# A two-layer graph network on one core: attention masks made by two DMAs, one bias added by an accumulating DMA, weights fetched through a ring

## The chip, the cores and the metric

The kernel runs on one core of one Trainium2 chip. Its time is the device time of one execution in microseconds. The core has five engines that each work through their own queue in order: TensorE (PE in the profile, its weight loads are PEld), VectorE (DVE), ScalarE (ACT), GpSimd (POOL) and SyncE (SP, which here only issues DMAs). DMAs are issued from SP's queue and from POOL's queue.

## The reference

There are 32 graphs of 512 nodes with 256 features, and one 0/1 adjacency matrix of 512x512 per graph, given as int32, in which one entry in 32 is set. Two layers follow each other, each of a graph part and a feed-forward part, all with layer norm in front and a residual sum behind:

```python
# layer 0
x = x + relu(xn @ W_upd + (adj^T @ (xn @ W_msg)) / degree + bias)
t = max over d of (xn[d] + Wt[:, d]) + bt                  # tropical product, 1024 units
fused = g * pieces(t) + (1 - g) * gelu(xn @ Wc + bc)       # g = sigmoid(xn @ Wg + bg)
x = x + fused @ Wd + bd
# layer 1
score[i, j] = leaky_relu(src[i] + dst[j]) where adj[i, j] is 1, else excluded   # 4 heads of 64
x = x + layer_norm(relu(softmax_j(score) @ h + bias) + h) * gamma + beta
x = x + slice_mixer(xn)                                    # softmax to 64 slices x 8 heads, a scan, back
```

What matters below: layer 1's attention needs the mask of each graph with the node j of the sum on the partitions, that is `adj` transposed; and `bd`, the last bias of layer 0, is one row of 256 that is added to every node.

## The kernel before

**Layer 0** (`layer0_sorted`, lines 98 to 702). The graph convolution of each graph loads `adj` by a casting DMA from POOL's queue (line 392). The tropical product is not computed in full: rows are sorted by how many features can still win, and for each such feature a row of a table in DRAM is fetched by an indirect DMA on POOL's queue (lines 564 and 595, 128 rows of 4 KB each) and taken into a running maximum on DVE (line 598). `sums(s, g)` does this for a group of four tiles of 128 rows; there are 32 groups. Its last step adds `bd`, held in SBUF on all partitions, to the group's rows `xg`: four POOL instructions of 128x256 (line 610). `mixed` is the matmuls of the feed-forward part (line 623) and its pieces (lines 628 to 641), and `down` is the last product, added to `xg` (line 654) and stored to `x2s` (line 655, SP's queue).

**Layer 1** (`layer1_plain`, lines 865 to 1611) is a generator. Its setup is woven into the last groups of layer 0 by `woven`, a step at a time. The setup loads and transposes the weights: `load_T` (line 999) loads 128 rows of a weight by SP's queue into one of two buffers, transposes them on PE (line 1009) and copies them out on ACT (line 1010); there are 21 such steps. The last setup steps are `masks(0)`.

`masks(b)` (line 1080) makes the mask of graph b in four tiles of 128 rows. For each tile SP loads 256 KB of int32 (line 1086), ACT casts it to bf16 with a sum (line 1100) and squares it in place with a sum (line 1101), PE transposes four blocks of 128x128 (line 1091), and DVE copies them out of PSUM as uint8 (line 1092). The two sums serve the check at the end of `layer1_plain` (lines 1607 to 1611): every entry must be 0 or 1, and every row must have an edge. A flag that is raised there makes `tile_kernel` run both layers again in a plain form (line 2212).

`prepare(b)` (line 1155) gathers the rows of graph b (line 1161), runs `masks(b)` in between, norms (line 1173), adds a row by an accumulating DMA (`add_rows`, line 949, POOL's queue), makes the projections `hp` (line 1187), and brings the factors of the nodes i onto all partitions by way of DRAM: `ownd` (line 1204) and four loads `own` (line 1207), all on SP's queue. It has 15 steps (`STEPS`). `weigh` (line 1215) makes the attention weights on DVE: `max(own, other) * mask`, 16 instructions of 128x512 for each graph (line 1220). `attention(b)` (line 1223) multiplies them on PE: for each j, 8 products `avp` (line 1256), then 4 row sums `adp` (line 1261), in the order of the heads. While graph b is attended, `prepare(b + 1)` is woven in, and the slice mixer of the two graphs before runs beside both, at a pace (`PACE`, line 896) that is worked out from `TURNS`, `STEPS` and `WANTED`.

The order within each engine's queue is not the order of the source alone: the framework moves instructions of the same queue past one another where no data forbids it, and gives each DMA one of eight completion counters per kind of queue, which it waits for when it is used again.

Of the kernel before, what the change touches and what calls it, by code (L numbers as in the profile page):

```python
# [8 lines left out]
F32 = mybir.dt.float32  # L9
F32R = mybir.dt.float32r  # L10
I32 = mybir.dt.int32
BF16 = mybir.dt.bfloat16
# [7 lines left out]
P = 128  # L20
# [77 lines left out]
def layer0_sorted(tc, ident, eps, x, adj, w, x2s, ranks, over, following):  # L98
# [29 lines left out]
    with ExitStack() as ctx:  # L128
# [12 lines left out]
        bd = const("bd", [P, D], w["bd"].partition_broadcast(P))  # L141
# [35 lines left out]

        table = dr.tile([D, FFN], F32, tag="table", name="table", bufs=1)
# [364 lines left out]
        def feed_forwards():  # L543


            def sums(s, g):
# [62 lines left out]
                for t in range(NT):  # L609
                    nc.gpsimd.tensor_add(xg[:, t, :D], xg[:, t, :D], bd)  # L610
# [254 lines left out]
def layer1_plain(tc, ident, eps, x2s, ranks, adj, w, out, over, ps):  # L865
# [24 lines left out]
    STEPS = 15  # L890
# [10 lines left out]
    with ExitStack() as ctx:  # L901
# [16 lines left out]
        identb = cst.tile([P, P], BF16, tag="identb", name="identb")  # L918
        nc.vector.tensor_copy(identb, ident)
# [32 lines left out]
        edges = ctile("edges", [P, 2, B * NT])  # L952
# [44 lines left out]
        with tc.tile_pool(name="raw", bufs=2, side="right") as raw:  # L997

            def load_T(dst, src, name):

                R, Ccols = src.shape
                for r0 in range(0, R, P):
                    n = min(P, R - r0)
                    t = raw.tile([P, Ccols], F32, tag=f"raw{Ccols}", name=f"{name}_{r0}")
                    nc.sync.dma_start(t[:n], src[r0 : r0 + n, :])
                    pt = psum("tp", f"{name}p{r0}").rearrange("p (c r) -> p c r", r=P)
                    cs = Ccols // P
                    for c in range(cs):
                        nc.tensor.transpose(pt[:, c, :n], t[:n, c * P : (c + 1) * P], ident[:n, :n])
                    nc.scalar.copy(dst[:, :, r0 : r0 + n], pt[:, :cs, :n])  # L1010
                    yield

            yield from load_T(wfxT, w["W_fx"], "wfx")
            yield from load_T(inT, w["hy_in_w"], "in")
            yield from load_T(hoT, w["hy_out_w"], "ho")
            yield from load_T(owT, w["out_w"], "ow")
            yield from load_T(fcT, w["hy_fcD_w"], "fc")
# [5 lines left out]
            def twice_T(src, name):  # L1023

                R, Ccols = src.shape
                t = raw.tile([P, 2, Ccols], F32, tag="twice", name=name)
                for i in range(2):
                    nc.sync.dma_start(t[:R, i, :], src)
                pt = psum("tp", f"{name}p")
                nc.tensor.transpose(pt[:, :R], t[:R].rearrange("p i c -> p (i c)"), ident[:R, :R])  # L1030
                return pt


            wsT = raw.tile([P, G], F32, tag="wsT", name="wsT")
            nc.vector.tensor_copy(wsT, twice_T(w["W_slice"], "ws")[:, :G])
            wx = raw.tile([P, KC, D], F32, tag="wx", name="wx", bufs=1)
            nc.sync.dma_start(wx, w["W_x"].rearrange("(k p) d -> p k d", p=P))
            bx = raw.tile([P, KC], F32, tag="bx", name="bx")
            nc.sync.dma_start(bx, w["b_x"].rearrange("(k p) -> p k", p=P))
            bsl = raw.tile([1, H, G], F32, tag="bsl", name="bsl", bufs=1)  # L1040
            bs = raw.tile([1, G], F32, tag="bs", name="bs")
            nc.sync.dma_start(bs, w["b_slice"].rearrange("(o n) -> o n", o=1))
# [22 lines left out]
            for c in range(DC):  # L1065
                sq = raw.tile([P, H * G], F32, tag="wsl2", name=f"wsl2_{c}")
                nc.vector.tensor_mul(sq, wsl[:, c, :], wsl[:, c, :])
                nc.tensor.matmul(pn, ones, sq, start=c == 0, stop=c == DC - 1)
# [9 lines left out]
        masked = {}  # L1078

        def masks(b, bank="any"):  # L1080

            a, raw = [], []

            def load(t):
                raw.append(se.tile([P, N], I32, tag="ai", name=f"ai{b}_{t}", bufs=2))
                nc.sync.dma_start(raw[t], adj[b, t * P : (t + 1) * P, :])

            def turn(t):
                pt = ps.tile([P, NT, P], BF16, tag=bank, name=f"maskp{b}_{t}")
                for j in range(NT):  # L1090
                    nc.tensor.transpose(pt[:, j, :], a[t][:, j * P : (j + 1) * P], identb)
                nc.vector.tensor_copy(mask[:, :, t * P : (t + 1) * P], pt)

            load(0)
            load(1)
            yield
            for t in range(NT):
                n = b * NT + t
                a.append(se.tile([P, N], BF16, tag="a", name=f"a{b}_{t}", bufs=3))
                nc.scalar.activation(a[t], raw[t], AF.Identity, accum_out=edges[:, 0, n : n + 1])  # L1100
                nc.scalar.activation(raw[t], raw[t], AF.Square, accum_out=edges[:, 1, n : n + 1])
                if t + 2 < NT:
                    load(t + 2)
                if t == 1:
                    mask = se.tile([P, NT, N], mybir.dt.uint8, tag="mask", name=f"mask{b}")
                    yield
                if t > 1:
                    turn(t - 2)
                    yield
            for t in range(NT - 2, NT):  # L1110
                turn(t)
                yield
            masked[b] = mask

        yield from masks(0, "mm")
# [39 lines left out]
        def prepare(b):  # L1155
# [12 lines left out]
            edged = masks(b) if b not in masked else range(3)  # L1168
            for i, _ in enumerate(edged):
                if i < 3 or b not in masked:  # L1170
                    yield
                if i == 2:
                    normed(xt, xn, f"c{b}")
                    add_rows(xt, 0)
                    yield
# [5 lines left out]
            ht = sb.tile([P, NT, AH * HO], F32, tag="ht", name=f"ht{b}")  # L1181
            other = sb.tile([P, NT, AH], F32, tag="other", name=f"other{b}")
# [40 lines left out]
        def attention(b):  # L1223
# [21 lines left out]
            for i, (q, j) in enumerate(turns):  # L1245
# [5 lines left out]
                if q + 1 == AP:  # L1251
                    ends = dict(start=j == 0, stop=j == NT - 1)
                    for p in range(AP):
                        for k in range(2 * HO // HW):
                            h, e = 2 * p + k * HW // HO, k * HW % HO
                            nc.tensor.matmul(pv[p][k * HW : (k + 1) * HW, :], hv[:, j, h, e : e + HW],  # L1256
                                             weighed[b, h, j], **ends)
                    if j == 0:
                        pd = psum("pv", f"adp{b}")
                    for h in range(AH):  # L1260
                        nc.tensor.matmul(pd[h * HW : (h + 1) * HW, :], hv[:, j, h, HO:].to_broadcast([P, HW]),
                                         weighed.pop((b, h, j)), **ends)
# [14 lines left out]
            nc.vector.tensor_scalar_max(rs, dt.rearrange("p (t h e) -> p t h e", t=NT, h=AH)[:, :, :, 0], 1e-30)  # L1277
            nc.vector.reciprocal(rs, rs)
# [329 lines left out]
        nc.vector.tensor_sub(flags, edges[:, 1, :], edges[:, 0, :])  # L1608
        nc.vector.tensor_scalar(flags, flags, 0.0, None, ALU.not_equal)
        nc.vector.tensor_scalar(edges[:, 0, :], edges[:, 0, :], 0.5, None, ALU.is_lt)  # L1610
        nc.vector.tensor_add(flags, flags, edges[:, 0, :])
# [635 lines left out]
```

## Time and profile before

| what | us |
|---|---|
| median of three runs | 4365.9 (4364.42 to 4366.94) |
| the profiled execution, its own time | 4372.35 |
| its span, first to last instruction | 4370.6 |
| PE busy | 3882.4 (89% of the span) |
| DVE busy | 3279.3 (75%) |
| ACT busy | 2295.0 (53%) |
| POOL busy | 1617.9 (37%) |

The span is read as four stretches: layer 0 until about 1860 us after its start; the last groups of layer 0 with the setup of layer 1 woven in, until about 2340; the passage, until about 2520; and layer 1 proper, in which two graphs take some 120 us and which ends at 4370.6. A group's "idle before" is time in which its engine stood still ahead of it, with what ended the wait. Busy times of different engines overlap and do not add up to the span.

### The profile page before, as it was taken

How to read it: one execution, taken by the hardware profiler on the slowest of the kernel's cores; microseconds unless marked ns; L12 is line 12 of the kernel's file. 1: busy time of each engine (PE TensorE's matmuls, PEld its weight loads, DVE VectorE, ACT ScalarE, POOL GpSimd, SP SyncE). 2: the span in 40 equal slices, each digit the busy share in tenths (PEclk: the TensorE clock that was granted, in tenths of full speed). 3: DMA queues.
4: the chain of work that ended last, by engine and by line, in shares of the span. 5: the costliest groups of instructions: out<-in, count | busy, mean ns of one | idle time of the engine just before them, and what ended most of it. 6: DMA issues, size and time to landing. Idle time of an engine off the chain costs nothing.

```text
span 4370.6 us, 57973 instructions
## 1 busy us (share of the span) xinstructions
PE 3882.4 (89%) x20311; PEld 2456.1 (56%) x20311; DVE 3279.3 (75%) x7008; ACT 2295.0 (53%) x4756; POOL 1617.9 (37%) x2036
## 2 busy tenths in 40 slices
PE   5567898988989999888998899999999999999997
PEld 4454565565655666554555455655555555555555
DVE  6668887898878978877775777777777777777763
ACT  3345655566655656546564555555554455554533
POOL 2346644665536644354431322222222222222210
PEclk8778999999999999998999999999999999999998
DMA  5546543564436644375441322222222322222200
GB/s 128 160 154 216 179 156 126 165 218 143 153 117 199 199 156 135 93 250 167 147 133 40 95 73 73 69 65 72 68 68 76 78 75 78 64 74 77 61 25 21
DMA packets 244051, 507.52 MB, mean 116 GB/s; under 512 B 39299, under 2 KB 114827, under 8 KB 243748
## 3 DMA queue, kind: packets, MB, share of 16 engines
q0 software_dynamic: 107904, 349.50, 26.7%
q1 hardware_dynamic: 135844, 154.21, 11.3%
q8 instruction: 162, 2.65, 0.2%
q14 instruction: 141, 1.16, 0.1%
HBM read 446.46 MB, written 57.17 MB: 115 GB/s over the span
## 4 chain that ended last, share of the span: by engine, by line
DVE 33%; PE 32%; DMA 11%; issue 9%; POOL 8%; ACT 5%; SPq 0%; another core or an unknown queue 0%; DVEq 0%; POOLq 0%; ACTq 0%
DVE att L1220 4%; DVE acc L637 4%; PE clsp L623 4%; PE gatep L623 3%; PE po L652 3%; PE avp L1256 3%; DMA rows<-table,xs 2%; DVE best L598 2%; DMA rows<-table,tops 2%; DVE sw L1349 2%; DVE sst L1347 2%; PE yTp L1354 2%; DVE sw L1344 2%; PE oTp L1542 1%; DMA best<-table,xs 1%
## 5 line engine op out<-in xcount | busy, mean ns | idle before, releaser
L623 PE MATMUL clsp<-xnT,wc 128*128 128x512 f32 x1024 | 521.8, 628 | 55.5 <-ACT cls L625 39.7
L623 PE MATMUL gatep<-xnT,wg 128*128 128x512 f32 x1024 | 502.1, 609 | 10.5 <-ACT gate L625 9.7
L652 PE MATMUL po<-wd,acc 128*128 128x256 f32 x2048 | 456.9, 382 | 6.5 <-DVE acc L641 3.5
L652 PEld LDWEIGHTS po<-wd,acc 128*128 128x128 f32 x2048 | 388.8, 191 | 73.1 <-issue 9.2
L1220 DVE SCALAR_TENSOR_TENSOR att<-own,other,mask 128x512 f32<-128x512 f32 x512 | 366.1, 744 | 76.4 <-DMA own<-ownd 76.4
L637 DVE SCALAR_TENSOR_TENSOR acc<-past,fld,acc 128x512 f32<-128x512 f32 x448 | 346.3, 776 | 28.3 <-ACT past L636 20.3
L598 DVE SCALAR_TENSOR_TENSOR best<-rows,xs,best 128x1024 f32<-128x1024 f32 x212 | 273.1, 1290 | 121.4 <-ACT best L592 75.8
L632 ACT ACTIVATE acc<-tz,fld 128x512 f32<-128x512 f32 x256 | 199.0, 778 | 269.1 <-PE tz L630 237.5
L623 PEld LDWEIGHTS gatep<-xnT,wg 128*128 128x128 f32 x1024 | 197.3, 197 | 254.0 <-issue 200.8
L636 ACT ACTIVATE past<-tz,fld 128x512 f32<-128x512 f32 x448 | 291.6, 694 | 73.6 <-DVE acc L637 72.1
L595 POOL DMA_INDIRECT rows<-table,xs x212 | 247.3, 1166 | 176.7 <-DVE best L598 121.8
L1256 PE MATMUL avp<-att,hv 128*32 128x512 f32 x2048 | 297.4, 599 | 6.1 <-DVE att L1220 6.1
L623 PEld LDWEIGHTS clsp<-xnT,wc 128*128 128x128 f32 x1024 | 182.6, 199 | 195.2 <-issue 114.3
L434 PE MATMUL pm<-h,adj 128*128 128x258 f32 (+1 forms) x1024 | 178.9, 321 | 100.3 <-DVE keep L427 34.4
L625 ACT ACTIVATE gate<-gatep,fld 128x512 f32<-128x512 f32 x256 | 175.6, 686 | 153.4 <-PE gatep L623 130.4
L1342 PE MATMUL lgp<-wsl,x4T 128*128 128x512 f32 x512 | 241.4, 610 | 14.3 <-ACT sw L1343 6.7
L1354 PE MATMUL yTp<-sw,x 128*128 128x512 f32 x512 | 237.0, 602 | 17.4 <-DVE sw L1349 16.9
L1161 POOL DMA_INDIRECT x<-x2s,ranks x128 | 135.2, 1056 | 295.5 <-DVE att L1220 147.5
L553 POOL DMA_INDIRECT xs<-rows_of,order x128 | 158.8, 1241 | 229.7 <-DVE acc L637 111.8
L1307 POOL TENSOR_TENSOR mu<-mu,eps 128x16 f32<-128x16 f32 x32 | 111.3, 3478 | 350.4 <-DVE mu L1306 350.4
L1574 PE MATMUL outp<-v,swT 128*128 128x256 f32 x1024 | 227.6, 381 | 0.0
L625 ACT ACTIVATE cls<-clsp,fld 128x512 f32<-128x512 f32 x256 | 176.3, 689 | 94.4 <-PE clsp L623 59.1
(598 smaller groups left out, 8809.0 us busy)
## 6 DMA issues: line engine op xcount, KB each, us to landing
adj<-in_adj POOLq DMA_DIRECT2D x128, 256.0 KB
ai<-in_adj SPq DMA_DIRECT2D x128, 256.0 KB
x<-added POOLq DMA_DIRECT2D x64, 512.0 KB
own<-ownd SPq DMA_DIRECT2D x128, 256.0 KB
rows_of<-keep SPq DMA_DIRECT2D x32, 550.0 KB
x<-in_x SPq DMA_DIRECT2D x32, 512.0 KB
x2s<-xs SPq DMA_DIRECT2D x32, 512.0 KB
out<-x SPq DMA_DIRECT2D x32, 512.0 KB
```

The source lines that it names most:

```text
L595: nc.gpsimd.indirect_dma_start(out=row, out_offset=None, in_=table, in_offset=bass.IndirectOffsetOnAxis(ap=idxs[:, k : k + 1].bitcast(U32) ...
L598: nc.vector.scalar_tensor_tensor(m, row, vals[:, k : k + 1], m, ALU.add, ALU.max)
L623: nc.tensor.matmul(pf, wf[:, c, f * P : (f + 1) * P], xnT[:, c, :], start=c == 0, stop=c == DC - 1)
L625: nc.scalar.activation(o, pf, fn, bias=fld[:, f, bf : bf + 1], scale=1.0 if fn == AF.Gelu else 0.5)
L636: nc.scalar.activation(r, z, AF.Relu, bias=fld[:, f, AT + b : AT + b + 1])
L637: nc.vector.scalar_tensor_tensor(y, r, fld[:, f, CH + b : CH + b + 1], y, ALU.mult, ALU.add)
L652: nc.tensor.matmul(po[:, i, :], acc[f][:, t * P : (t + 1) * P], wd[:, f, :], start=f == 0, stop=f == FC - 1)
L1220: nc.vector.scalar_tensor_tensor(e, own[h], other[:, j, h : h + 1], mask[:, j, :], ALU.max, ALU.mult)
L1256: nc.tensor.matmul(pv[p][k * HW : (k + 1) * HW, :], hv[:, j, h, e : e + HW], weighed[b, h, j], **ends)
L1342: nc.tensor.matmul(pf, xnT[:, c, t * P : (t + 1) * P], wsl[:, c, :], start=c == 0, stop=c == DC - 1)
L1354: nc.tensor.matmul(py, xn[:, t, c * P : (c + 1) * P], sw[:, t, :], start=t == 0, stop=t == NT - 1)
L1574: nc.tensor.matmul(po[:, :D], swT[:, k, t * P : (t + 1) * P], v[:, k, :], start=k == 0, stop=k == KC - 1)
```

## The change

Four edits, made together.

1. **Masks.** `masks` is gone, with its loads, casts, squares, transposes and copies. In its place `shorten(b)` copies the adjacency matrix of a graph from DRAM to DRAM by one DMA on POOL's queue that casts int32 to bf16 (1 MB read, 0.5 MB written), two graphs ahead and kept in the program's order; and `turn(b)` fetches it by one transposing DMA on SP's queue into a bf16 mask of 128x4x512. The check becomes one ACT instruction for each graph, the square of (mask - 0.5) over 128x2048 with a sum, which must be 512 on every partition, and one DVE instruction of 128x4 that looks for a row sum of the attention that is zero. `STEPS` is 12.
2. **Order in attention.** The 8 products and the 4 row sums of a step are issued from the last head to the first.
3. **bd.** It is copied four times into a row of DRAM, and each group adds it by one accumulating DMA of 128x4x256 on POOL's queue.
4. **Weights.** The weight rows of layer 1 go through a ring of five buffers that is filled three pieces ahead, and four small tensors are loaded before them.

```diff
-        bd = const("bd", [P, D], w["bd"].partition_broadcast(P))
+        bd = dr.tile([NT, D], F32, tag="bd", name="bd", bufs=1)
+        nc.sync.dma_start(bd, w["bd"].partition_broadcast(NT))
...
-                for t in range(NT):
-                    nc.gpsimd.tensor_add(xg[:, t, :D], xg[:, t, :D], bd)
+                nc.gpsimd.dma_start(xg[:, :, :D], bd.partition_broadcast(P), accum_op=ALU.add)
...
-    STEPS = 15
+    STEPS = 12
...
-            yield from load_T(wfxT, w["W_fx"], "wfx")
-            yield from load_T(inT, w["hy_in_w"], "in")
-            yield from load_T(hoT, w["hy_out_w"], "ho")
-            yield from load_T(owT, w["out_w"], "ow")
-            yield from load_T(fcT, w["hy_fcD_w"], "fc")
+            def fetch(i):
+
+                _, src, r0 = pieces[i]
+                n = min(P, src.shape[0] - r0)
+                t = raw.tile([P, DI], F32, tag="piece", name=f"piece{i}", bufs=5)
+                nc.sync.dma_start(t[:n, : src.shape[1]], src[r0 : r0 + n, :])
+                return t
+
+            coming = [fetch(i) for i in range(3)]
+            yield
+            for i, (dst, src, r0) in enumerate(pieces):
+                if i + 3 < len(pieces):
+                    coming.append(fetch(i + 3))
+                n, cs = min(P, src.shape[0] - r0), src.shape[1] // P
+                pt = psum("tp", f"piecep{i}").rearrange("p (c r) -> p c r", r=P)
+                for c in range(cs):
+                    nc.tensor.transpose(pt[:, c, :n], coming[i][:n, c * P : (c + 1) * P], ident[:n, :n])
+                nc.scalar.copy(dst[:, :, r0 : r0 + n], pt[:, :cs, :n])
+                yield
...
-        yield from masks(0, "mm")
+        short, masked = {}, {}
+
+        def shorten(b):
+
+            if b < B:
+                short[b] = dr.tile([N, N], BF16, tag="short", name=f"short{b}", bufs=3)
+                tc.keep_in_program_order(nc.gpsimd.dma_start(short[b], adj[b], max_dma_last_dim=8192))
+
+        def turn(b):
+
+            if b < B:
+                masked[b] = se.tile([P, NT, N], BF16, tag="mask", name=f"mask{b}")
+                nc.sync.dma_start_transpose(masked[b], short.pop(b))
+
+        for b in range(2):
+            shorten(b)
+            yield
+        turn(0)
...
-            edged = masks(b) if b not in masked else range(3)
-            for i, _ in enumerate(edged):
-                if i < 3 or b not in masked:
-                    yield
-                if i == 2:
-                    normed(xt, xn, f"c{b}")
-                    add_rows(xt, 0)
-                    yield
+            if b:
+                turn(b)
+            shorten(b + 2)
+            yield
+            yield
+            yield
+            normed(xt, xn, f"c{b}")
+            add_rows(xt, 0)
+            yield
...
             ht = sb.tile([P, NT, AH * HO], F32, tag="ht", name=f"ht{b}")
+            nc.scalar.activation(ht.rearrange("p t e -> p (t e)").bitcast(BF16), mask.rearrange("p t n -> p (t n)"),
+                                 AF.Square, bias=centre, accum_out=edges[:, b : b + 1])
...
-                    for p in range(AP):
-                        for k in range(2 * HO // HW):
+                    for p in reversed(range(AP)):
+                        for k in reversed(range(2 * HO // HW)):
...
-                    for h in range(AH):
+                    for h in reversed(range(AH)):
...
+            nc.vector.tensor_scalar(edges[:, B + b * NT : B + (b + 1) * NT],
+                                    dt.rearrange("p (t e) -> p t e", t=NT)[:, :, 0], 0.0, None, ALU.is_le)
```

## The prediction

> **What bounds the kernel now.** I read the busy time by stretch first, then the groups by line and form, the waits, the chain of waits, and last the SP and DVE timelines around one graph. The stretches (columns: length, PE, PEld, DVE, ACT, POOL busy with instructions, PE clock, DMA share, GB/s):
>
> ```profile
> 300.00:1860.00 1560.00, 1389.03 (x5548) 908.04 (x5547) 1294.39 (x2618) 915.76 (x1572) 839.21 (x1123) 0.96 0.51 162
> 1860.00:2000.00 140.00, 116.16 (x438) 72.63 (x437) 101.36 (x137) 70.65 (x115) 76.05 (x65) 0.87 0.68 230
> ...
> 2520.00:4200.00 1680.00, 1609.38 (x10865) 974.95 (x10865) 1246.80 (x2805) 862.53 (x2212) 420.62 (x385) 1.00 0.26 70
> ```
>
> Layer 1 proper is PE's: 1609 of 1680 us, 96%, against 74% for DVE, 51% for ACT, 25% for POOL and a DMA share of 0.26. Layer 0 is nobody's alone: PE 89%, DVE 83%, POOL 54%, DMA 51%. Between 1860 and 2000 us PE falls to 83%. The groups that the change removes, and the accumulating DMA that stands as a model for the new one:
>
> ```profile
> L1091 PE MATMUL maskp<-identb,a 128*128 128x128 bf16 x512 | 45.4, 220 | 13.9 <-ACT sw L1343 8.5 <-DVE mask L1092 4.5 <-ACT a L1100 0.9
> L1092 DVE CAST mask<-maskp 128x512 uint8<-128x512 bf16 x128 | 85.8, 676 | 0.4
> L1100 ACT ACTIVATE a<-ai 128x512 bf16<-128x512 int32 x128 | 80.6, 630 | 94.5 <-PE maskp L1091 70.0 <-PE outp L1574 13.6 <-DMA ai<-in_adj 10.7
> L1101 ACT ACTIVATE ai<-ai 128x512 int32<-128x512 int32 x128 | 81.6, 638 | 1.2
> L610 POOL TENSOR_TENSOR xs<-xs,bd 128x256 f32<-128x256 f32 x128 | 109.3, 859 | 165.9 <-ACT xn L574 164.8
> L949 POOL DMA_DIRECT2D x<-added x64 | 59.5, 930 | 260.4 <-ACT x L1140 129.8 <-ACT hv L1140 117.8 <-ACT avT L1273 10.1
> ```
>
> On PE the masks cost little beside the matmuls, on DVE and ACT more. How much of this sets the end is read from the chain between 3000 and 3130 us (start, us, what):
>
> ```profile
> 3010.86 0.33 PE maskp L1091 x4
> ...
> 3026.12 0.67 PE maskp L1091 x12
> ...
> 3075.53 0.60 DVE mask L1092
> ...
> 3081.95 0.60 DVE mask L1092
> ...
> 3089.96 0.60 DVE mask L1092
> ...
> 3093.18 0.56 DVE mask L1092
> ```
>
> Six mask pieces, 3.36 us in 130, lie on it. Over the whole span the chain gives DMA 11% and POOL 8%:
>
> ```profile
> DVE 33%; PE 32%; DMA 11%; issue 9%; POOL 8%; ACT 5%; SPq 0%; another core or an unknown queue 0%; DVEq 0%; POOLq 0%; ACTq 0%
> ```
>
> **What the Trainium skill says.** (1) "DMA: Bandwidth & Descriptors", section SWDGE vs HWDGE vs iDMA: a cast or an accumulate needs GpSimd's queue, a transpose SP's or ACT's. The trace agrees as far as it goes: line 392's casts and line 949's accumulates are POOL's. No transposing DMA is in it. (2) The same page, Queues, rings and completion order: SP owns one ring on each DMA engine, and on an engine descriptors are consumed in order. So an `own` load issued behind a transposing DMA comes after it. (3) "VectorE: DVE Perf Modes", The three transpose paths: 390 ns for a block of 128x128 on TensorE, 1309 ns by DMA. The trace has 220 ns for PE's, 56 ns apart within a run (12 in 0.67 us).
>
> **The masks, removed.** For one graph 16 transposes, 4 copies, 8 ACT instructions with their sums, 4 loads. On the chain 3.36 us in 130 us are 3.1 us for two graphs (some 120 us), and with 30 of the 31 graphs made in this stretch that is 15 x 3.1 = 47 us. PE alone gives the same size: 512 x 0.056 = 29 us if only the pitch counts, 45.4 + 13.9 = 59 us with its own busy time and the idle before it. I take 47. Late next are PE's own matmuls and DVE's `att`. ACT loses 128 x (0.630 + 0.638) and two sums of about 0.2 each, some 213 us. It is not the bound, and PE's weight loads waited only 7.5 (`yTp`) and 10.9 us (`gp`) for its casts: I take -5 (0 to -18).
>
> **The masks, new work.** ACT: a row of 512 takes 0.63 us and one of 1024 takes 1.05 (line 1303), so 2048 come to about 1.9 + 0.2: 32 x 2.1 = 67 us of ACT, covered by its 49% idle; without the cover it is 67. DVE: 32 comparisons of 0.15 us, 5 us, set against 86 that leave. `att` reads bf16 in place of uint8; I leave its 0.74 us. POOL: 32 casting DMAs at 0.57 to 0.93 us of issue are 18 to 30 us. POOL's part of the chain is 8% of 4370 = 350 us of 1618 busy, 22%, so +6; it stands ahead of the next gather, the norms and `hv`. The casting DMA moves what the four `ai` loads moved, so its DMA time replaces theirs.
>
> **The transposing DMA** is the open price. From below: 0.5 MB at the 261 GB/s which the DMA page (Latency and other measured facts) gives, 2 us. From above: 16 blocks x 1.309 = 21 us if they follow each other; with 3.4 us to land, as `ownd` has, 24. I take 6 and keep both. It waits for the last `att` of two graphs before, since there are two mask buffers, and on SP's queue it stands right ahead of the next `ownd` and `own`. The timelines of DVE and SP show how much room there is:
>
> ```profile
> 3029.90 0.74 DVE L1220 SCALAR_TENSOR_TENSOR att<-own,other,mask 128x512 f32<-128x512 f32 x1
> 3057.65 0.75 DVE L1220 SCALAR_TENSOR_TENSOR att<-own,other,mask 128x512 f32<-128x512 f32 x1 [7.21 <-DMA own<-ownd]
> ```
>
> ```profile
> 3050.76 0.33 SPq L1204 DMA_DIRECT2D ownd<-turned  x1
> 3054.24 1.75 SPq L1207 DMA_DIRECT2D own<-ownd  x4
> ```
>
> The last `att` ends at 3030.6, `ownd` is issued at 3050.8: 20.1 us. Read so for graphs 2 to 31 the room is 12.9 to 27.7 us, 21.4 in the mean. At 6 us nothing is delayed. The square on ACT comes half an attention later, and until then the mask has landed; were it late, ACT would hold `hp`'s copies behind it. I add +3 for SP's longer issue.
>
> **bd.** 128 additions of 0.859 us leave POOL, 32 DMAs of 0.93 come: 109 - 30 = 79 us less, of which 22% on the chain, -17. The new DMA's price: one `added` transfer kept the DMAs at 0.15, 1.07, 1.07 and 0.37 in four successive microseconds from 3104, 2.6 us of all 16 engines. 32 of them are 85 us, amid the row gathers. The chain's share of DMA time is 11% of the span over a mean busy share of 0.38, 29%: +25. Against that, the four additions held POOL's queue 165 us waiting for ACT (`xn`), with gathers behind them; one wait for each group stays. I take 16 off for it, so -8 in all; the ends are -79 (all of POOL's time counts) and +85 (all of the DMA time counts).
>
> **Weights.** PE waited for weight rows 7.4 us (`in`), 4.1 (`wfx`) and 3.2 (`ho`), 14.7 in all, while ACT's and DVE's waits behind it overlap. Three pieces ahead cover them: -10 (0 to -25). The two casts that now fall into these groups stand in POOL's queue ahead of a gather: 2 x 3 us of DMA, half of it in place of the `ai` loads: +3.
>
> **Order of heads.** The first product now waits for the weight that is made last, and 11 that follow wait for none. The weights are made three turns ahead, and PE waited 6.1 us for them in all: 0 (-6 to +3).
>
> **Sum.** -47 - 5 + 6 + 3 - 8 - 10 + 3 = -58, against the profiled execution's own 4372.35 (the span's 4370.6 and 1.8 around it): 4314. The median lies 6.5 under that execution, so 4308.
>
> **Rivals.**
> A slow transposing DMA (slower). If it takes D from issue to landing, each `own` is late by what D is over its room. Added over the 30 graphs that is 2 us at D = 15, 49 at 21, 109 at 24, 259 at 30. It decides from D = 21.5, where 58 is used up. At the block price, 24, the time is 4308 + 109 = 4417. For it: nothing here shows D, and `att` already idles 76.4 us for `own`. Against it: the bandwidth price is a tenth.
> POOL is the hidden bound of layer 0. Its queue feeds gathers that stand on the chain, and 165 us of waits go. With -79 in place of -8 the time is 4237. Against it: PE and DVE are at 89% and 83% there.
> The gain is given back. The accumulating DMAs fall into bursts of gathers, of which 512 KB follow each other every 1.2 us: +60 in place of +25, and of the layer 1 gain only PE's 29 counts: 4308 + 35 + 18 = 4361.
> The change doesn't do what it says: if the square of 0.5 isn't exactly 0.25 in ACT's sum, the check raises the flag and both layers run again, at least twice the time. Nothing suggests it.
>
> **Numbers.** Forecast, 4270 to 4345: 0.63. POOL: 0.11. Slow transpose: 0.13. Given back: 0.11, of which half ends within 0.2%. Flag: 0.02. Faster 0.63 + 0.11 + 0.04 = 0.78, same 0.05, slower 0.13 + 0.02 + 0.02 = 0.17; 0.2%, 9 us, is about what a measurement of this kernel can tell from no change. The range takes in POOL's and the given-back case and leaves out most of the slow transpose and the flag: 4240 to 4385.
>
> **What would show it.** Two graphs in layer 1 should take about 117 us in place of 120, with PE at 96% or more; the transposing DMA should land well before `ownd`; POOL's waits at line 610 should fall below 100 us and the waits of DVE for row gathers (43.6 and 39.5 us) should not double; PE's waits for weight rows should vanish. I am wrong if `att` waits for `own` much over 76 us, if ACT waits at the square, or if layer 0 becomes longer.

## The result, and the profile after

The changed kernel takes 4343.7 us (median of 12 runs, 4332.9 to 4362.92), the kernel before beside it 4365.16 (12 runs, 4348.12 to 4372.6). The ratio is 0.9958, 95% interval 0.9942 to 0.9974: 18 us less, between 11 and 25. The forecast was 58 us less, 4308. The time lies in the forecast's range, but less than a third of the gain came. By its number it lies between the forecast and the case "the gain is given back" (4361), but it is not that case, which put the loss on the accumulating DMAs of layer 0 and left 29 us of gain in layer 1.

The profiled execution of the changed kernel is the fastest of its twelve (4332.9, span 4331.2), so the two traces differ by 39.4 us, more than the medians do. What follows reads where the time went inside the two traces, and takes sizes from the timed runs.

The same three stretches as before (length, then PE, PEld, DVE, ACT and POOL busy with their instructions, PE clock, DMA share, GB/s), in the changed kernel:

```profile
300.00:1860.00 1560.00, 1410.67 (x5629) 923.89 (x5629) 1268.16 (x2599) 922.48 (x1579) 779.64 (x1045) 0.96 0.57 174
1860.00:2000.00 140.00, 116.38 (x468) 69.93 (x468) 118.05 (x165) 79.26 (x126) 80.80 (x61) 0.95 0.80 250
...
2520.00:4200.00 1680.00, 1568.10 (x10251) 942.94 (x10250) 1181.25 (x2691) 766.46 (x1799) 451.05 (x410) 0.98 0.31 69
```

In layer 1 the masks are gone from PE, DVE and ACT, but PE is now busy for 1568 us of 1680, not 1609: it has less to do and stands idle more. Its clock is 0.98 (1.00 before). The groups that came, and the one whose wait the prediction named:

```profile
L1164 ACT ACTIVATE ht<-mask,centre 128x2048 bf16<-128x2048 bf16 x32 | 64.1, 2002 | 71.7 <-DVE mu L1292 49.9 <-DMA x2s<-xs 17.1 <-issue 4.6
L610 POOL DMA_DIRECT2D xs<-bd x32 | 44.6, 1395 | 83.7 <-ACT xn L575 59.3 <-issue 14.1 <-ACT cls L625 10.1
L1085 POOL DMA_DIRECT2D short<-in_adj x32 | 19.5, 614 | 0.1
L1142 POOL DMA_INDIRECT x<-x2s,ranks x128 | 151.4, 1183 | 334.4 <-DMA out<-x 118.5
```

POOL's wait at line 610 fell from 164.8 to 59.3 us. The row gathers of layer 1 (line 1142) now wait 118.5 us for `out`, the store of finished rows; before, 3.1 us of their waits between 2520 and 4150 us were put down to that store. The chain of waits, by engine, has PE up (32% before) and DVE down (33%):

```profile
PE 40%; DVE 21%; DMA 11%; issue 9%; POOL 7%; ACT 4%; POOLq 0%; DVEq 0%; SPq 0%; ACTq 0%
```

Where the time went: the first `att` starts at 2363.6 us (2421.2 before), so all that lies ahead of it became 57.6 us shorter; from there to the end it takes 1967.6 us (1949.4 before), 18.2 us **longer**. Below, "layer 1" means this stretch. The prediction had most of its gain there.

One pair of graphs shows what happened. POOL's queue in the changed kernel (start, us, what, in brackets the idle time ahead and its end):

```profile
3617.08 0.61 POOL L1085 DMA_DIRECT2D short<-in_adj  x1
...
3626.38 1.07 POOL L1142 DMA_INDIRECT x<-x2s,ranks  x1 [4.84 <-DMA out<-x]
3627.75 0.96 POOL L1142 DMA_INDIRECT x<-x2s,ranks  x1 [0.30 <-issue]
3628.74 2.93 POOL L1294 TENSOR_TENSOR mu<-mu,eps 128x16 f32<-128x16 f32 x1
```

DVE and PE in the same microseconds:

```profile
3622.87 0.75 DVE L1204 SCALAR_TENSOR_TENSOR att<-own,other,mask 128x512 f32<-128x512 f32 x1
3631.70 1.23 DVE L1297 TENSOR_TENSOR av<-av,mu 128x1024 f32<-128x1024 f32 x1 [8.09 <-POOL mu L1294]
...
3634.64 1.29 DVE L1331 TENSOR_TENSOR sw<-sw,ebsl 128x512 f32<-128x512 f32 x2
```

```profile
3630.93 1.16 PE L1171 MATMUL hp<-wa,x3T 128*128 128x264 f32 x4
3638.10 10.28 PE L1341 MATMUL yTp<-sw,x 128*128 128x512 f32 x16 [6.01 <-DVE sw L1336]
```

Read from the top. The gather needs a row buffer that the `out` store, issued at 3618.2, must first have emptied. It stands at the head of POOL's queue until 3626.4. Behind it stands `mu`, a power of 128x16 for the norm of the attention (DVE had delivered its input at 3623). DVE has nothing ahead of `av` in its queue and waits 8.1 us; behind `av` stands the softmax of the slice mixer (`sw`), and for that PE waits 6.0 us. In the kernel before, a gather of that place started 4.4 us after its store, `mu` started as soon as its input was there (3680.5, ready at 3684.3), and DVE had work queued ahead of `av`: the mixer's softmax and two mask copies. It did not wait at all:

```profile
3680.30 1.22 DVE L1308 TENSOR_TENSOR av<-av,gamma 128x1024 f32<-128x1024 f32 x1
3681.44 1.30 DVE L1344 TENSOR_TENSOR sw<-sw,ebsl 128x512 f32<-128x512 f32 x2
...
3684.08 1.28 DVE L1349 TENSOR_TENSOR sw<-sw,sst 128x512 f32<-128x512 f32 x2
3685.28 1.28 DVE L1092 CAST mask<-maskp 128x512 uint8<-128x512 bf16 x2
3686.48 1.22 DVE L1310 TENSOR_TENSOR av<-av,mu 128x1024 f32<-128x1024 f32 x1
```

What covered `mu` there is the softmax: it ends at 3685.4, a microsecond after `mu`, and the two copies come only then. In all 14 such places of the trace before, `av` starts 2.1 to 6.7 us after `mu` has ended, more than the 1.3 us that two copies take. In the changed kernel `av` stands ahead of the softmax in ten of the pairs; there `mu` starts 2.3 to 6.5 us late and DVE waits 4.6 to 8.8 us. In three pairs the softmax still stands ahead, and DVE waits 0.7 us at most, though in two of them `mu` starts 2.6 us late:

```profile
3047.54 1.22 DVE L1297 TENSOR_TENSOR av<-av,mu 128x1024 f32<-128x1024 f32 x1 [0.68 <-POOL mu L1294]
```

So the loss has two parts: `mu` comes later, and the order of DVE's queue no longer hides it.

The stall has a second price. The clock in four stretches of the changed kernel around it (columns as in the stretches above):

```profile
3618.20:3630.00 11.80, 11.44 (x56) 4.66 (x52) 4.81 (x12) 8.31 (x14) 4.53 (x5) 1.00 0.57 115
3630.00:3637.20 7.20, 2.09 (x16) 0.77 (x8) 5.50 (x9) 0.57 (x4) 6.68 (x5) 1.00 0.19 44
3637.30:3644.10 6.80, 6.00 (x7) 2.36 (x8) 6.80 (x19) 0.00 (x0) 0.00 (x0) 0.50 0.91 146
3644.10:3654.00 9.90, 9.90 (x50) 5.92 (x52) 2.87 (x14) 6.17 (x23) 2.44 (x4) 1.00 0.28 55
```

For 6.8 us after the stall PE gets half its clock. The 16 products took 10.28 us; in the kernel before, 8 of the same took 3.70, so 16 take 7.4. The Trainium skill, "TensorE: Matmul & The Clock Gate", Part 1 (The HAM clock gate), describes this: an activity monitor gives half the clock after an idle window of about 3.4 us, and the full clock after a busy one. The trace agrees: PE had stood still since 3632.1 when its clock fell at 3637.3. Of the 13 stretches of half clock in the 14 pairs from the first `out` store to the 29th, twelve last 3.4 or 6.8 us and one 13.7. Over these pairs, the clock records of the changed kernel hold 78 us at half clock, those of before 17.

### The profile page after: what moved, and what is told of

It is laid out like the page before. It is cut to its first block, busy times and chain, and to the rows that moved or that the text cites. A ratio compares the mean times of both kernels' runs of the same rounds, so it can differ in the third digit from the quotient of the medians.

```text
span 4331.2 us, 56115 instructions
## 1 busy us (share of the span) xinstructions
PE 3835.0 (89%) x19799; PEld 2420.8 (56%) x19799; DVE 3174.6 (73%) x6909; ACT 2189.0 (51%) x4308; POOL 1578.4 (36%) x1973
## 4 chain that ended last, share of the span: by engine, by line
PE 40%; DVE 21%; DMA 11%; issue 9%; POOL 7%; ACT 4%; POOLq 0%; DVEq 0%; SPq 0%; ACTq 0%
PE yTp L1341 4%; PE clsp L623 4%; PE gatep L623 4%; PE avp L1241 4%; PE po L652 3%; DVE att L1204 3%; DVE acc L637 3%; DMA rows<-table,xs 2%; PE lgp L1329 2%; DVE best L599 2%; PE adp L1246 2%; DMA out<-x 2%; DMA best<-table,xs 1%; PE xp L1394 1%; PE oTp L1529 1%
## 5 line engine op out<-in xcount | busy, mean ns | idle before, releaser
L637 DVE SCALAR_TENSOR_TENSOR acc<-past,fld,acc 128x512 f32<-128x512 f32 x448 | 332.0, 743 | 30.7 <-ACT past L636 22.9
L596 POOL DMA_INDIRECT rows<-table,xs x212 | 257.6, 1215 | 188.0 <-DVE best L599 122.0
L1341 PE MATMUL yTp<-sw,x 128*128 128x512 f32 x512 | 253.5, 642 | 59.5 <-DVE sw L1336 59.3
L1241 PE MATMUL avp<-att,hv 128*32 128x512 f32 x2048 | 257.7, 605 | 23.8 <-DVE att L1204 23.8
L1142 POOL DMA_INDIRECT x<-x2s,ranks x128 | 151.4, 1183 | 334.4 <-DMA out<-x 118.5
```

Source lines behind the costliest of these rows:

```text
L596: nc.gpsimd.indirect_dma_start(out=row, out_offset=None, in_=table, in_offset=bass.IndirectOffsetOnAxis(ap=idxs[:, k : k + 1].bitcast(U32) ...
L637: nc.vector.scalar_tensor_tensor(y, r, fld[:, f, CH + b : CH + b + 1], y, ALU.mult, ALU.add)
L1341: nc.tensor.matmul(py, xn[:, t, c * P : (c + 1) * P], sw[:, t, :], start=t == 0, stop=t == NT - 1)
```

## The experiments

Each run was timed in five rounds against the kernel before, in five sets of two to four kernels (median of before 4364 to 4372); differences are the ratio less one times that median, with the 95% interval. "Layer 1" is from the first `att` to the end, in the profiled execution. Versions whose layer 1 is about equally long (1926 us) came to -53 and -58 in one set and to -75 in another, so differences of some 15 us between sets aren't read.

| run | us | against before | layer 1 |
|---|---|---|---|
| the kernel before | 4365.2 | | 1949.4 |
| the changed kernel | 4343.7 | -18 (-25 to -11) | 1967.6 |
| b_bd | 4350.5 | -22 (-29 to -16) | 1953.0 |
| b_ring | 4360.8 | -10 (-14 to -5) | 1948.1 |
| b_masks | 4405.1 | +33 (+26 to +40) | 1980.4 |
| b_order | 4367.8 | -4 (-8 to -1) | 1943.6 |
| b_none | 4322.3 | -45 (-51 to -38) | 1952.4 |
| a_steps15 | 4341.5 | -28 (-35 to -21) | 1955.8 |
| a_free | 4402.3 | +28 (+19 to +36) | 1939.0 |
| a_dump | 4358.8 | -14 (-18 to -10) | 1964.3 |
| a_nosq | 4332.0 | -28 (-35 to -21) | 1961.8 |
| a_x6 | 4297.2 | -75 (-83 to -68) | 1925.6 |
| a_late | 4343.9 | -18 (-25 to -11) | 1961.7 |
| a_late_x6 | 4305.5 | -57 (-63 to -50) | 1933.7 |
| a_gpin | 4427.0 | +63 (+55 to +71) | 2042.0 |
| a_gpin_x6 | 4454.6 | +86 (+78 to +95) | 2082.2 |
| a_x6_dump | 4301.0 | -58 (-67 to -49) | 1927.4 |
| a_x6_steps15 | 4314.1 | -53 (-61 to -45) | 1926.3 |
| b_x6 | 4388.5 | +19 (+12 to +25) | 1964.8 |
| b_masks_x6 | 4339.3 | -31 (-37 to -24) | 1925.6 |

**The four edits alone.** Each is applied to the kernel before as the diff above has it. `b_bd`:

```diff
-                for t in range(NT):
-                    nc.gpsimd.tensor_add(xg[:, t, :D], xg[:, t, :D], bd)
+                nc.gpsimd.dma_start(xg[:, :, :D], bd.partition_broadcast(P), accum_op=ALU.add)
```

> The kernel before with the third edit alone (bd by an accumulating DMA). The prediction's sum gives it -8 us. The rival that POOL is the hidden bound of layer 0 gives about -20 to -30, since the trace of the changed kernel stored group 16 of layer 0 some 23 us sooner, where only this edit was at work. If the DMA price is paid in full, it is +10 to +40. Layer 1 should keep its length (some 1949 us from the first att to the end) in each theory.

`b_ring`:

```diff
-            yield from load_T(wfxT, w["W_fx"], "wfx")
...
+            coming = [fetch(i) for i in range(3)]
```

> The kernel before with the fourth edit alone (weights through a ring of five). The prediction's sum gives it -10 us (0 to -25). If the 26 us that the changed kernel gained between groups 16 and 25 are the ring's, it gives about -25. If they come from the masks that left the setup, it gives -5 or less.

`b_masks`:

```diff
-        yield from masks(0, "mm")
+        for b in range(2):
+            shorten(b)
+            yield
+        turn(0)
```

> The kernel before with the first edit alone (masks by casting and transposing DMAs, square on ACT, 12 steps). The prediction's sum gives it -47 - 5 + 6 + 3 + 3 = -40 us, all but the first 3 in layer 1. If the masks themselves are what failed, it comes to between 0 and +20 us, with layer 1 some 15 to 20 us longer than the 1949 of before, and the same waits as in the changed kernel: DVE av waits for POOL's mu about 100 us (20 before), POOL's x gather waits for the out store. If the order of heads is what failed, layer 1 is here shorter by 30 us or more.

`b_order`:

```diff
-                    for h in range(AH):
+                    for h in reversed(range(AH)):
```

> The kernel before with the second edit alone (products and row sums of the attention from the last head to the first). The prediction's sum gives it 0 us (-6 to +3). The rival that the reversed order makes the first product wait for the weight made last gives +15 to +40, with avp waiting for DVE's att 20 us or more (6 before).

The ring gave the 10 us of the sum and the order of heads about nothing, -4. bd gave 22, not 8. The masks alone cost 33 us where the sum had a gain of 40, and layer 1 is 31 us longer with them, with the same waits as in the changed kernel: DVE's `av` waits 97 us for `mu` (20 before). So the masks edit is what failed. The four differences add up to -3; together the edits give -18. These 15 us are no more than two sets can differ by, but layer 1 is also 13 us shorter in the changed kernel than with the masks alone. The order of heads may be what does it: alone it takes PE's busy time over the 14 pairs from 1591.8 to 1578.4 us.

**What in the masks: weave, cast order, square, buffers.** Four runs on the changed kernel. `a_steps15` restores the old number of steps:

```diff
-    STEPS = 12
+    STEPS = 15
...
             add_rows(xt, 0)
             yield
+            yield
+            yield
+            yield
```

> The changed kernel with 15 steps in prepare in place of 12: three empty ones more where the mask pieces stood, so that the weave and the pace of layer 1 are those of before. If the shifted weave is what ate the gain (DVE's last norm of the attention then stands ahead of the mixer's softmax and waits for POOL's mu, 97 us of av waits against 20 before), layer 1 shortens from 1967 us to about 1905 (1949 less the 47 of the prediction), the time is about -75 to -80 against before, and DVE's waits for mu fall below 30 us. If POOL's queue or the square itself is the cause, layer 1 stays within 10 us of 1967 and the time near -18.

`a_free`:

```diff
-                tc.keep_in_program_order(nc.gpsimd.dma_start(short[b], adj[b], max_dma_last_dim=8192))
+                nc.gpsimd.dma_start(short[b], adj[b], max_dma_last_dim=8192)
```

> The changed kernel, with the casting DMA not kept in the program's order. If the pinned place of the cast in POOL's queue delays mu, DVE's waits for mu fall from 98 us to below 40 and the time is about -50 against before. If the weave or the wait of the gathers for the out store is the cause, nothing changes: -18 +-7.

`a_dump`:

```diff
-            nc.scalar.activation(ht.rearrange("p t e -> p (t e)").bitcast(BF16), mask.rearrange("p t n -> p (t n)"),
+            nc.scalar.activation(hv.rearrange("p t h e -> p (t h e)")[:, : NT * N // 2].bitcast(BF16), mask.rearrange("p t n -> p (t n)"),
                                  AF.Square, bias=centre, accum_out=edges[:, b : b + 1])
```

> The changed kernel with the square's unused result written into hv, not into ht, so that ACT doesn't wait for DVE's reading of ht by the norm of two graphs before (47 us of waits, 27 times). If that wait ahead of hp's copies is the cause, the time falls by 20 to 45 us against the changed kernel (-40 to -60 against before). If POOL's mu is what counts, by less than 10.

`a_x6`:

```diff
-    AHEAD_X = 2 * GB + 1
+    AHEAD_X = 2 * GB + 2
```

> The changed kernel with six buffers for the rows x in place of five, so that POOL's row gathers don't wait for the out store of a graph five before (118 us of waits, 16 times, with mu queued behind them). If that wait is what makes mu late, DVE's waits for mu fall from 98 us to below 40 and the time is -45 to -65 against before. If the weave is the cause, mu is late in another place and the time stays near -18 (-10 to -30).

`a_x6` beats both kernels: 4297.2, and 42 us of layer 1 come back. DVE's waits for `mu` fall from 98 to 56 us, not below 40, but none is longer than 3.1 us (8.8 with five). One pair of it, beside one of the changed kernel in which the stall stands (columns as above):

```profile
3603.70:3719.70 116.00, 109.33 (x730) 66.31 (x726) 83.57 (x194) 55.04 (x131) 33.76 (x31) 1.00 0.31 73
```

```profile
3618.20:3740.10 121.90, 113.34 (x742) 67.85 (x738) 84.36 (x194) 55.17 (x131) 32.34 (x30) 0.97 0.32 70
```

For about the same work PE is busy 4.0 us longer in the second, at a clock of 0.97, and idle 1.9 us longer. The forecast's 117 us for two graphs is met with six buffers, though PE is busy for 94% of them, not 96%.

The edit does two things at once. `AHEAD_X` is the number of buffers, and `prepare` also has a loop at its head that doesn't begin a graph until the graph `AHEAD_X` before it is stored; with six, the program may place the gathers earlier, too. The run doesn't separate the two.

The old weave is worth 12 us of layer 1, not 60: that theory falls as the main cause. But `a_steps15` also shows that the waits don't measure the loss. DVE waits 39 us for `mu` in it, and POOL 21 us for the `out` store, both less than with six buffers (56 and 52), and yet its layer 1 is 30 us longer. It still has 65 us at half clock over the 14 pairs; six buffers have 34. The square's place is worth 3.

`a_free` missed in a way that teaches something: left to the framework, all 32 casts were issued in the first 90 us of the kernel, where they held up layer 0's own loads (the first store of rows came at 508 us, not 417). Layer 1, now without any cast, is 29 us shorter than in the changed kernel, against 42 with six buffers. So the casts do have a part in the loss, and perhaps most of it; no run has both remedies.

**Is it the collision of the cast with the store?** In the packets of the trace, a pair's second `out` store (0.5 MB) ended 2.6 to 4.2 us after its issue before the change. In the changed kernel it ended 6.3 to 7.2 us after it wherever the cast of 1 MB had gone 1.2 us ahead. `a_late` moves the cast away from it, `a_late_x6` does both, `a_nosq` takes the square away, and `b_none` leaves bd out to price that edit. `a_late`:

```diff
-            shorten(b + 2)
             yield
...
                                  abias.rearrange("p (h e) -> p h e", h=AH).unsqueeze(1).to_broadcast([P, NT, AH, HO]))
+            shorten(b + 2)
```

> The changed kernel with the casting DMA issued later in prepare, behind the addition that makes hv, where no out store and no row gather is under way; five row buffers as before. In the changed kernel the cast goes 1.2 us ahead of a pair's second out store, whose last packet then ends 6.3 to 7.2 us after its issue (2.9 before), and the gather for that buffer starts 8 us after it (4.4 to 7.7 before). If this collision is the cause, the store ends after 3 us again, DVE's waits for mu fall from 98 us below 50, layer 1 shortens from 1967 to 1915-1935, and the time is -50 to -70 against before. If five buffers are too few in any case, it stays near -18 to -25.

`a_late_x6` has `AHEAD_X = 2 * GB + 2` besides:

> Both: the cast issued later and six row buffers. If the collision is the whole cause, the sixth buffer adds less than 10 us to what the later cast gives. If the wait for the store costs by itself, this is 20 us or more below the later cast alone. With six buffers alone the time was -75 against before; if cast and buffers take away different waits, it is -85 to -100.

`a_nosq`:

```diff
+        nc.gpsimd.memset(edges[:, :B], 0.25 * NT * N)
...
-            nc.scalar.activation(ht.rearrange("p t e -> p (t e)").bitcast(BF16), mask.rearrange("p t n -> p (t n)"),
-                                 AF.Square, bias=centre, accum_out=edges[:, b : b + 1])
```

> The changed kernel without the square of the mask on ACT: it leaves out the test that every entry of the adjacency is 0 or 1 (its sums are set to the value that passes). The prediction has the square covered by ACT's idle time: then the time stays within 10 us of the changed kernel's (-18 against before). If ACT's queue behind the square is part of the loss, it is -35 to -60.

`b_none`:

```diff
-                for t in range(NT):
-                    nc.gpsimd.tensor_add(xg[:, t, :D], xg[:, t, :D], bd)
```

> The kernel before with the addition of bd left out altogether (its rows then lack this bias). The prediction's sum takes 17 us of POOL work on the chain and 16 us of waits away: -33. The accumulating DMA alone was measured at -22 in all. If this run is at -33, the DMA costs 11, not the 25 of the sum; if it is at -22, the DMA costs nothing and the removal was priced too high; if at -47, the price of 25 was right and the removal was priced too low.

With the later cast nearly every store ended after 2.6 us again, as expected; but DVE still waited 69 us for `mu`, 75 us for `own` (26 in the changed kernel, the cast being now beside those loads), and layer 1 was only 6 us shorter. A wait of 4.4 us on DVE was still enough for half clock. PE was busy for 1.3 of the 3.6 us before it, with one gap of 2.3 us (columns as above):

```profile
3646.40:3650.00 3.60, 1.29 (x5) 0.59 (x4) 3.60 (x9) 0.57 (x4) 1.01 (x2) 1.00 0.66 132
3650.00:3656.90 6.90, 5.89 (x8) 1.97 (x7) 5.82 (x18) 0.38 (x1) 1.23 (x2) 0.51 0.15 29
```

So the collision made the wait longer, but taking it away didn't bring the gain back; as the later cast made another wait longer, the run doesn't price the collision alone. With six buffers the later cast gained nothing (layer 1 is 8 us longer than with six buffers alone). Without the square layer 1 is 6 us shorter, and the whole perhaps 10, which the intervals don't separate from none. Leaving bd out gives -45; with the DMA, -22. So the DMA costs some 22, within what two sets can tell.

**Is it `mu`'s place behind the gather?** `a_gpin` keeps the gathers in the program's order and one step later, so that `mu` stands ahead of the second gather of a pair. The transposing and the casting DMA of that step stay where they were, and so come ahead of the gathers now:

```diff
+            if b:
+                turn(b)
+            shorten(b + 2)
+            yield
             for t in range(NT):
-                nc.gpsimd.indirect_dma_start(
+                tc.keep_in_program_order(nc.gpsimd.indirect_dma_start(
...
-            if b:
-                turn(b)
-            shorten(b + 2)
-            yield
```

> The changed kernel with the row gathers kept in the program's order and one step later in prepare; five row buffers. mu then stands ahead of the second gather of a pair in POOL's queue. If mu behind the waiting gather is what ate the gain, DVE's waits for mu fall from 98 us below 30, PE's clock in layer 1 rises from 0.98 to 0.99 or 1.00, layer 1 shortens from 1967 us to 1925-1945, and the time is -40 to -60 against before. If the rows simply come too late with five buffers, DVE waits for the gathers instead (32 us now) and the time stays at -10 to -25.

`a_gpin_x6`:

> The same with six row buffers. If the wait of mu is the one cause, the sixth buffer adds little to the pinned gathers, and the time is near that of six buffers alone: -65 to -85 against before. If buffers and order count each for itself, it is below -85.

`a_x6_dump` and `a_x6_steps15` are the edits shown above, with six buffers:

> Six row buffers, and the square's unused result written into hv in place of ht. With five buffers the place of the square's result made no difference. If ACT's wait for ht (60 us with six buffers) was hidden there by the longer wait for mu, it gives 10 to 20 us now, -85 to -95 against before; else the time is that of six buffers alone, -75 +-10.

> Six row buffers and 15 steps in prepare. With five buffers the 15 steps gave 12 us of layer 1. If they did so by making mu come earlier, they give less than 5 with six buffers (-70 to -80 against before); if the old weave is better in itself, -85 to -95; if it only fitted the masks on PE, -50 to -65.

`a_gpin` is inconclusive on its question, and so is `a_gpin_x6`, which missed by the most (+86 where -65 or less was expected; DVE waited 123 us for rows). In `a_gpin` the waits for `mu` fell to 43 us, but the second gather of a pair now started some 33 us after the store, DVE waited 107 us for rows (35 in the changed kernel), and layer 1 became 74 us longer. It shows how much hangs on the rows' coming early; it doesn't show that `mu`'s place alone would have been worth the 42 us. `a_x6_dump` and `a_x6_steps15` added nothing to six buffers. The latter has a second reading: beside `a_steps15`, the sixth buffer makes layer 1 29 us shorter although DVE's waits for `mu` rise from 39 to 47 us; the time at half clock over the 14 pairs falls from 65 to 20 us. So what the sixth buffer gives doesn't all pass through `mu`.

**Would six buffers have helped the kernel before as much?** They didn't fit there, so both of these runs have one attention buffer fewer:

```diff
-    ATT = 2 * (AHEAD + 2) + AP + 1
+    ATT = 2 * (AHEAD + 2) + AP
...
-    AHEAD_X = 2 * GB + 1
+    AHEAD_X = 2 * GB + 2
```

> The kernel before with six row buffers in place of five, and 12 attention buffers in place of 13 to make room. In the kernel before the av waits for mu are 20 us in all and PE's clock in layer 1 is 0.99 to 1.00, so if the wait for the out store became costly only with the new masks, this is within 10 us of before. If a sixth buffer helps any version, it is -30 to -45.

> The same two sizes, with the first edit (masks) alone. With five buffers the masks alone cost 33 us. If the masks are worth the 40 us of the prediction once the rows don't come at the last moment, this is 30 to 45 us below the kernel before with six buffers. If the masks lose by something else (casts, transposes, the square), it stays 10 us or more above it.

They would not: the kernel before became 19 us slower. (Which of the two sizes did that isn't separated; `own` was waited for 102 us, 76 before.) With the same two sizes the masks edit is 49 us **faster** than without it (4388.5 to 4339.3; the two intervals together allow 40 to 58). With five buffers it is 33 us slower. In the traces layer 1 is 39 us shorter with it than without; 15 of them are what the two sizes had made it longer, so against the kernel before it is 24. In layer 1 proper its PE is busy as long as before, with the mask pieces gone from it:

```profile
2520.00:4200.00 1680.00, 1611.15 (x10651) 970.76 (x10652) 1214.05 (x2775) 790.11 (x1858) 455.05 (x411) 1.00 0.30 69
```

1611 us of 1680, 10,651 matmuls where the changed kernel did 10,251 in the same window, at full clock. (The window holds somewhat different work, as the 14 pairs begin at 2583 us here and at 2532 in the changed kernel. They take 1631 us here, 1682 there and 1668 before.)

## Why the prediction was right or wrong

**Wrong: "The masks, removed", -47, "Late next are PE's own matmuls and DVE's att".** The work was there to be had, about as priced. Over the 14 pairs PE's busy time is 1591.8 us before and 1549.4 with six buffers, 42 less: 13 of them came with the order of heads alone, and 30 with the masks (1594.5 to 1564.4 between the two runs with 12 attention buffers), as the lower of the two prices for PE, 29, has it. With six buffers the masks edit gains 49.

What the step got wrong is what comes late next. It was neither of the two that it named, but the softmax of the mixer, for which PE waits 59 us between 2520 and 4150 us, 15 before. In the pair shown it stands behind `av`, that behind `mu`, and `mu` behind a gather that needs a buffer at the last moment. The changed kernel's sum over the 14 pairs is: busy 1570.0 us, 21 more than with six buffers (its 44 us more at half clock cost about 22), and idle 111.9, not 75.9: 36 more than before. Together +14 where -42 was to be had.

The step failed in its method: it took the mask pieces out of the chain of waits and let everything else stand. On DVE the softmax had stood ahead of `av` and hidden `mu`'s way through POOL. With the masks gone the framework put the queue in another order, with `av` ahead of the softmax in most pairs, and the cover was gone just where `mu` became later. What sets this order isn't shown. A clock that falls after a stall stood nowhere in the sum. That five row buffers decide between loss and gain is shown by the runs; that the loss goes by way of `mu` is read from the traces, and `a_steps15` doesn't fit it fully.

**Wrong: "The casting DMA moves what the four `ai` loads moved, so its DMA time replaces theirs", POOL +6.** The bytes are the same, the moment isn't. The four loads followed the `out` store on SP's queue; the cast is one burst of 1 MB on POOL's, beside the store or beside `own`. Without any cast in it, layer 1 is 29 us shorter, and moving the cast moved the wait to `own`. The +6 for POOL counted issue time; the instruction's issue is the small part (0.61 us each).

**Mis-sized: bd, -8; measured -22.** The DMA was priced at +25, and the two runs give some 22. The removal was priced at 17 + 16 = 33, and leaving bd out gave 45 (38 to 51). So the mis-sized term is POOL's, by some 12 us: its wait at line 610 fell by 105 us in the changed kernel, and the rival "POOL is the hidden bound of layer 0", which had -79, was right in direction. Which of POOL's waits the 12 are isn't shown. It was the cost of the DMA that kept the gain small.

**Right: the transposing DMA, 6 us, and the slow transpose refuted.** All 32 landed in a median of 4.3 us (4.1 to 13.6) after their issue, and `att` waited less for `own` than before (27 us, 76 before). The Trainium skill's price of 1309 ns for a block of 128x128 by DMA ("VectorE: DVE Perf Modes", The three transpose paths) would have made 21 us of the sixteen blocks. The room, though, was misread: the 12.9 to 27.7 us run from the last `att` of the graph just before to `ownd`, not from that of two graphs before, which frees the mask's buffer. In the changed kernel each transposing DMA is issued as that one ends, 43 to 87 us ahead of the `ownd` of its graph. So at 24 us the slow case would have held up no `ownd`, where the prediction put 109 us on it.

**Right: the weights' ring, -10 (measured -10), and the order of heads, 0 (-4).** The waits for weight rows didn't vanish, but fell from 14.7 us to 5.8 (3.5 of them at `in`'s rows, 7.4 before).

**Nearly right: the square on ACT, covered.** It took 2.00 us and a sum of 0.19, as priced. That ACT waits at the square was named as a sign of being wrong, and it does, 72 us, 50 of them for DVE's reading of `ht`; yet the square's place changed layer 1 by 3 us and its absence by 6.

What stays open: whether `mu`'s place alone, with the rows arriving as early as they did, would give the 42 us; it wasn't isolated. Nor is it known what else of layer 1 the sixth buffer helps, as it does with 15 steps, or how much of the 42 us would come without the casts. It isn't settled either why six buffers cost the kernel before 19 us.

## What to carry to other kernels

When an edit takes work out of an engine's queue, don't count on the rest to keep its order: list the waits that are hidden now because other work stands ahead of them, and ask what each would cost if it came to light. A buffer that is refilled at the very moment when its last user's store lands makes every instruction behind the refill late; here one more buffer gave some 57 us on top of the change's 18, 42 of them in layer 1, and the change had made the room for it. And a stall of PE by a few microseconds counts twice where the clock falls after it.

## What the runs showed of the hardware

- A PE that was idle for 5.1 of 7.2 us got half its clock for the next 6.8 us (changed kernel). In `a_late` 2.3 idle microseconds of 3.6 had the same effect. In the pair shown PE was busy 4 us longer than in one without the stall, 113.3 us against 109.3.
- A store of 0.5 MB behind a casting DMA of 1 MB that another queue issued 1.2 us sooner ends 6.3 to 7.2 us after its issue, in place of 2.6 to 4.2.
- 32 casting DMAs of 1 MB from DRAM to DRAM, issued back to back within 90 us, ended at 109 us; in the first 100 us PE was busy for 10, in the changed kernel for 52.
- The square of 128x2048 bf16 took ACT 2.00 us. An accumulating DMA of 128x4x256 from one row in DRAM took POOL 1.40 us to issue (0.93 for one of 128x1024) and 6.7 us to land.
